# Rearranging the start and the tail of a fused attention and feed-forward block

## The chip, the cores and the metric

The kernel runs on one core of one Trainium2 chip. A core has five engines that run side by side: TensorE (PE in the profile; PEld is its weight load) multiplies matrices, VectorE (DVE) and ScalarE (ACT) do element work and can read the matmul results in PSUM, GpSimd (POOL) does element work in SBUF alone, and SyncE (SP) issues transfers. Each engine takes its instructions in the order in which the program lists them and waits at the first that isn't ready. The metric is the time of one execution on the device in microseconds (us).

## The reference, cut to what matters

The input x has 8 batches of 1024 rows and 256 columns. Everything is float32. From a small condition c come six rows per batch, used as shifts, scales and gates:

```python
mod = (silu(c) @ wmod).reshape(8, 6, 1, 256)
sa, ca, ga, sb, cb, gb = (mod[:, j] for j in range(6))
ga, gb = (sign(g) * maximum(abs(g), 0.25) for g in (ga, gb))   # sign of 0 is +1
h = layernorm(x) * (1 + ca) + sa
scores = einsum('nsd,ntd->nst', h * w_lhs, h * w_rhs)
x = x + ga * einsum('nst,ntd->nsd', softmax(scores, axis=2), h)
h = layernorm(x) * (1 + cb) + sb
x = x + gb * (relu(h @ W1 + b1) @ W2 + b2)                     # 256 -> 1024 -> 256
```

## The kernel before, in words

Rows are worked in tiles of 128, and tiles in halves of four: a batch b has eight tiles i and two halves g. One main loop runs over the batches and, within each, over the tiles. At step (b, i) it forms the scores of a tile two steps ahead and multiplies the finished weights of tile i with the values. From batch 1 on, each step also carries a share of the feed-forward of the half batch before. Batch 0 has no such work to mix in, and the last half batches are finished after the loop, in the tail.

**Statistics and normalised x.** `prepare_stats` takes mean and variance of a tile (two VectorE instructions), `prepare_rstd` the inverse deviation of a half (two on ScalarE), and `prepare_norm` writes the normalised tile into `xg`. In batch 0 it uses VectorE for half 0's first two tiles and GpSimd for all others; later batches use ScalarE.

**Turned operands.** The scores need rows as columns. `prepare_turn` makes the left operand `lT` on VectorE and the right one `rT` on ScalarE from the turned tile, for both 128-column parts k of the 256. In batch 0 the turning is done by TensorE into PSUM tiles `pth`; in batch 1 `prepare_blocks` does it by VectorE's block transposes and a round trip of transfers through DRAM (T_a to D_a to X_a or Y_early), so `prepare_turn` reads SBUF there.

**Scores and weights.** `direct` multiplies `lT` and `rT` into `psc`, and ScalarE copies it to `sc`. Both weights multiply element by element, so the scores are symmetric and only the upper triangle is computed; `mirror` fills the rest, in batch 0 (`mirror_first`) by TensorE transposes `ptm` and ScalarE copies. `row_max` finds a row's maximum, `max_turn` turns it (`pm`), `subtract` (VectorE) and `exponent` (ScalarE) give the weights `pT`; `product` multiplies them with `xg` into `po`, and `product_out` divides, adds to x and takes statistics.

**Modulation.** `mod_rows` multiplies the condition with `wmod`; `mod_columns` turns two of its rows into columns in a PSUM tile `pmc`. From these come `sides` (scales and shifts of the two operands) and `modT` (those of the second normalisation); `make_gcol` and `columns` do the like for the gate's and the bias's columns. Eight small VectorE operations make the gated rows `rows_sb`, which `first_rows` spreads over all partitions (`prow`) for batch 0. They are also stored to DRAM for the later batches.

**Feed-forward.** `pair_products`, `pair_sums` and `pair_last` compute the first layer for a pair of 128-unit chunks (c and c+4) with fewer products than the plain form; `kept` is a ScalarE copy of one product that the pair needs before its last matmul. `pair_relu` follows. In the tail, `second` multiplies the second layer plainly: for each of four row tiles, eight matmuls over the chunks in the order 0, 4, 1, 5, 2, 6, 3, 7. The first three row tiles are split: a first part, and later the rest.

**What sets the order.** The order on each engine is the order of the calls: `pin` fixes it. PSUM has eight banks, in pools of two (`ps_s`), two (`ps_t`) and four (`ps_a`); a new tile waits until the last user of the bank it is given is done.

Of the kernel before, what the change touches and what calls it, by code (L numbers as in the profile page):

```python
# [17 lines left out]
P = 128  # L18
# [6 lines left out]
def adaln_block_kernel(  # L25
# [161 lines left out]
    def mod_rows(part, parts):  # L187

        pm = ps_a.tile([P, HALF], F32, tag="a", name=f"pmr_{part}")
        w = parts * D  # L190
        for k in range(ND):
            nc.tensor.matmul(
                pm[:B, :w],
                lhsT=scT[:, k, :],
                rhs=wm[:, k, ds(part * D, w)],
                start=(k == 0),
                stop=(k == ND - 1),
            )
        nc.scalar.copy(
            mod[:, part : part + parts, :].rearrange("b s d -> b (s d)"), pm[:B, :w]  # L200
        )

    def mod_columns(part):

        pc = ps_t.tile([P, HALF], F32, tag="t", name=f"pmc_{part}")
        for j in range(2):
            for k in range(ND):
                nc.tensor.transpose(
                    pc[:, ts(j * ND + k, B)], mod[:, part + j, ts(k, P)], ident[:B, :B]
                )  # L210
        return pc[:, : 2 * ND * B].rearrange("p (j k b) -> p j k b", j=2, k=ND)
# [55 lines left out]
    def prepare_rstd(b, g):  # L267
        pre[b, g].append(rstd_of(pre[b, g][0], "ra", f"ra_{b}_{g}"))

    def prepare_norm(b, g):  # L270

        mv, r = pre.pop((b, g))
        if b > 0:
            shift = work.tile([P, TH], F32, tag="rs", name=f"rs_{b}_{g}")
            nc.vector.scalar_tensor_tensor(shift, mv[:, :, 0], -1.0, r, ALU.mult, ALU.mult)
        for j in range(TH):
            t = g * TH + j
            if b > 0:
                nc.scalar.activation(
                    xg_t[b][:, t, 0:D], x_tile(b, t), AF.Identity,  # L280
                    scale=r[:, j : j + 1], bias=shift[:, j : j + 1],
                )
                continue
            engine = nc.vector if t < TH // 2 else nc.gpsimd
            engine.tensor_scalar(  # L285
                xg_t[b][:, t, 0:D], x_tile(b, t), mv[:, j, 0:1], r[:, j : j + 1],
                ALU.subtract, ALU.mult,
            )
# [57 lines left out]
    def prepare_turn(b, g, vector=True):  # L346

        xg, pts = xg_t[b], []
        lT = lT_t[b, g] = two.tile([P, ND, HALF], F32, tag="lT", name=f"lT_{b}_{g}", bufs=2)
        rT = rT_t[b, g] = two.tile([P, ND, HALF], F32, tag="rT", name=f"rT_{b}_{g}", bufs=2)  # L350
        rows = lambda T, k: T[:, k, :].rearrange("p (t a v) -> p t a v", a=NV, v=V)
        for k in range(ND):
            if b > 0:
                pt = pre[b, g][:, k]
            else:
                pt = ps_t.tile([P, HALF], F32, tag="t", name=f"pth_{b}_{g}_{k}")
                for j in range(TH):
                    nc.tensor.transpose(pt[:, ts(j, P)], xg[:, g * TH + j, ts(k, P)], ident)
                pt = pt.rearrange("p (t a v) -> p t a v", a=NV, v=V)
            pts.append(pt)  # L360
            if vector:
                nc.vector.tensor_scalar(
                    rows(lT, k), pt, side_col(0, 0, k, b), side_col(0, 1, k, b),
                    ALU.mult, ALU.add,
                )
            nc.scalar.activation(
                rows(rT, k), pt, AF.Identity,
                scale=side_col(1, 0, k, b), bias=side_col(1, 1, k, b),
            )
        def left():  # L370
            for k in range(ND):
                nc.vector.tensor_scalar(
                    rows(lT, k), pts[k], side_col(0, 0, k, b), side_col(0, 1, k, b),
                    ALU.mult, ALU.add,
                )

        return left


# [62 lines left out]
    def mirror_first(i):  # L442
        sc = first_scores()
        j = i + 1
        while j < NT:
            n = min(TH, NT - j)
            pt = ps_t.tile([P, HALF], F32, tag="t", name=f"ptm_{i}_{j}")
            for q in range(n):
                nc.tensor.transpose(pt[:, ts(q, P)], sc[:, i, ts(j + q, P)], ident)
            nc.scalar.copy(  # L450
                sc[:, j : j + n, ts(i, P)],
                pt[:, : n * P].rearrange("p (q s) -> p q s", s=P),
            )
            j += n
# [3 lines left out]
    def row_max(b, i):  # L458
        m = work.tile([P, 1], F32, tag="m", name=f"m_{b}_{i}")
        nc.vector.tensor_reduce(m, score_row(b, i), AX.XY, ALU.max)  # L460
        max_t[b, i] = m
# [431 lines left out]
    out_t = {}  # L893
    order = [i for c in range(NH) for i in (c, c + NH)]

    def second(b, a, parts=(0, 1), cut=NI // 2):

        w2g, f = ffn["w2g"], ffn["f"]
        if 0 in parts:
            out_t[a] = ps_a.tile([P, HALF], F32, tag="a", name=f"py_{b}_{a}")  # L900
        py = out_t[a]
        for i in (order[:cut] if 0 in parts else []) + (order[cut:] if 1 in parts else []):
            nc.tensor.matmul(  # L903
                py[:, :D],
                lhsT=f[:, i, ts(a % TH, P)],
                rhs=w2g[:, i, :],
                start=(i == order[0]),
                stop=(i == order[-1]),
            )
# [29 lines left out]
    prepare_stats(0, 1, range(2, TH))  # L939
    make_sides()  # L940
    prepare_rstd(0, 1)
    prepare_norm(0, 1)
    prepare_turn(0, 0)
    mod_rows(2, 1)
    mod_rows(5, 1)
    direct(0, 0, range(1))
# [15 lines left out]
    nc.vector.tensor_tensor(rows_sb[:, 3, :], gate[:, 1, :], b2_row, ALU.mult)  # L962


    left()
    rows_tile(0)
    rows_d = dram.tile([B, 4, D], F32, name="rows_d")
    nc.sync.dma_start(out=rows_d, in_=rows_sb)
# [48 lines left out]
    def make_gcol():  # L1017
# [5 lines left out]
                )  # L1023
        nc.scalar.copy(gcol.rearrange("p j k b -> p (j k b)"), pg[:, : 2 * ND * B])

    pr = first_rows()
    direct(0, 0, range(1, 2))
    keep_rows(pr, 0)
    direct(0, 1, range(1, 2))
    xg_half = lambda g: nc.vector.tensor_tensor(  # L1030
# [2 lines left out]
        rows_t[0][:, 0:1, :].to_broadcast([P, TH, D]),  # L1033
        ALU.mult,
    )
    xg_half(0)
    row_max(0, 0)
    mirror(0, 0)
    xg_half(1)
    keep_rows(pr, 1)  # L1040
# [6 lines left out]
    mirror(0, 1)  # L1047
    exponent(0, 0)
    mod_rows(3, 2)
    make_gcol()  # L1050
    max_turn(0, 1)
    subtract(0, 1)
    while queue:
        spare()
    columns(b1_rows, 0)


    modT = const.tile([P, 2, ND, B], F32, name="modT")
    pmb = mod_columns(3)
    nc.vector.tensor_copy(modT[:, 0], pmb[:, 0])  # L1060
    nc.vector.tensor_scalar(modT[:, 1], pmb[:, 1], 1.0, None, ALU.add)

    def early(b, i):

        if b == 0:

            if i in (1, 2):
                prepare_rstd(1, i - 1)
            elif i == 5:
                ffn_rstd(0, 0)  # L1070
            if i in (2, 3):
                prepare_norm(1, i - 2)
                x_plus(1, i - 2)
            if i in (3, 4):
                xg_times(1, i - 3)
            elif i == 5:
                prepare_turn(1, 0)
                sum_w2()
            elif i == 6:
                load_x(2, 0)  # L1080
        else:
            if i == 2 and b + 1 < B:
                prepare_norm(b + 1, 0)
            elif i == 6 and b + 2 < B:
                load_x(b + 2, 0)
# [22 lines left out]
    def norms(b, i):  # L1108
        if b > 0 and i == 0:
            ffn_blocks(b - 1, 1)  # L1110
        if b == 0:
            if i == 0:
                prepare_start(1)
                prepare_stats(1, 0)
            elif i == 1:
                prepare_stats(1, 1)
                sum_w1()
        elif b + 1 < B:
            if i == 1:
                prepare_start(b + 1)  # L1120
                prepare_stats(b + 1, 0)
            elif i == 2:
                prepare_blocks(b + 1, 0)
                x_plus(b + 1, 0)
                xg_times(b + 1, 0)
        elif i == 4:

            ffn_blocks(b, 0)
        if b == B - 1:
            return  # L1130
        if i == 6:
            if b == 0:
                ffn_norm(b, 0)
            ffn_blocks(b, 0)
# [7 lines left out]
    for b in range(B):  # L1142
        for i in range(NT):
# [25 lines left out]
            if b == 0:  # L1169
# [18 lines left out]
                spare()  # L1188
                if ahead[0] == 0:
                    subtract(*ahead)  # L1190
                norms(b, i)
                spare()
                if i == NT - 1:
# [9 lines left out]
            if first:  # L1203
# [7 lines left out]
                    pair_relu(c - 1)  # L1211
                pair_sums(fb, fg, c)
                if (b, i) == (1, 0):
                    weights(*late)
                    late = None
                if ahead:
                    mirror(*ahead)
                pair_last(fb, fg, c)
# [7 lines left out]
                if i == 4 and b + 1 < B:  # L1226
                    prepare_blocks(b + 1, 1)
                    xg_times(b + 1, 1)
                if late:
                    subtract(*late)  # L1230
                pair_products(fb, fg, c + 1, (lambda: max_turn(*extra)) if extra else None)
                if (b, i) == (B - 1, TH):
                    ffn_rstd(b, 0)
                if i == 5:
# [114 lines left out]
    for g in range(NT // TH):  # L1349
# [24 lines left out]
        tiles = range(g * TH, (g + 1) * TH)  # L1374

        for a in tiles[:3]:
            second(b, a, (0,), NI - 2)
        for a in tiles:
            second(b, a, (0, 1) if a == tiles[3] else (1,), NI - 2)
            second_out(b, a)  # L1380
            spare()
            spare()
# [40 lines left out]
```

## Time and profile before

| | |
|---|---|
| time, median of 3 runs | 768.08 us (767.98 to 768.21) |
| time of the profiled execution | 768.33 us |
| its span in the profile | 766.5 us |
| TensorE busy | 756.5 us, 99% of the span |
| VectorE, GpSimd, ScalarE busy | 566.4, 539.3, 374.9 us |
| granted TensorE clock | 1.0 of full speed |

The span runs from the first to the last recorded instruction. A row of a timeline or a group gives start or total in us, the engine, the line of the kernel, the operation, and in square brackets how long the engine stood idle before it and which instruction ended that. The chain of waits follows the work that ended last backwards, from each instruction to what released it.

### The profile page before, as it was taken

How to read it: one execution, taken by the hardware profiler on the slowest of the kernel's cores; microseconds unless marked ns; L12 is line 12 of the kernel's file. 1: busy time of each engine (PE TensorE's matmuls, PEld its weight loads, DVE VectorE, ACT ScalarE, POOL GpSimd, SP SyncE). 2: the span in 40 equal slices, each digit the busy share in tenths (PEclk: the TensorE clock that was granted, in tenths of full speed). 3: DMA queues.
4: the chain of work that ended last, by engine and by line, in shares of the span. 5: the costliest groups of instructions: out<-in, count | busy, mean ns of one | idle time of the engine just before them, and what ended most of it. 6: DMA issues, size and time to landing. Idle time of an engine off the chain costs nothing.

```text
span 766.5 us, 11489 instructions
## 1 busy us (share of the span) xinstructions
PE 756.5 (99%) x3708; PEld 621.8 (81%) x3708; DVE 566.4 (74%) x1222; ACT 374.9 (49%) x681; POOL 539.3 (70%) x632
## 2 busy tenths in 40 slices
PE   8999999999999999999999999999999999999998
PEld 3577789888887888878888888988888788888886
DVE  6697779668796887858787787866879677594632
ACT  4464545635465355555536444563546535251511
POOL 4633975978859697687867788597884879469641
PEclk9999999999999999999999999999999999999999
DMA  5314434356343653535544544436535354152220
GB/s 194 124 39 142 122 104 121 107 186 172 93 130 107 186 148 112 148 103 160 145 123 117 151 151 131 111 116 187 171 91 131 104 160 129 42 143 72 82 83 27
DMA packets 106212, 95.18 MB, mean 124 GB/s; under 512 B 29701, under 2 KB 98849, under 8 KB 106153
## 3 DMA queue, kind: packets, MB, share of 16 engines
q1 hardware_dynamic: 98408, 85.81, 38.9%
q10 hardware_dynamic: 7744, 8.65, 3.8%
q8 instruction: 29, 0.48, 0.3%
q14 instruction: 31, 0.25, 0.1%
HBM read 50.62 MB, written 43.81 MB: 123 GB/s over the span
## 4 chain that ended last, share of the span: by engine, by line
PE 95%; DVE 2%; POOL 1%; DMA 1%; issue 1%; ACT 1%; SPq 0%; POOLq 0%; DVEq 0%
PE po L493 16%; PE psc L410 16%; PE pa L718 10%; PE pb L718 7%; PE pc L718 7%; PE yc L798 6%; PE ya L798 6%; PE yb L798 6%; PE pr L584 5%; PE pq L584 3%; PE pp L544 3%; PE py L903 3%; PE yd L798 3%; PE pm L465 1%; POOL xg L285 1%; DMA x<-in_L_attn_x_dram 1%
## 5 line engine op out<-in xcount | busy, mean ns | idle before, releaser
L772 POOL TENSOR_TENSOR f<-f,kept 128x512 f32<-128x512 f32 x64 | 81.5, 1275 | 101.9 <-DVE f L771 96.8
L410 PE MATMUL psc<-rT,lT 128*128 128x512 f32 (+3 forms) x384 | 134.8, 487 | 0.0
L493 PE MATMUL po<-xg,pT 128*128 128x257 f32 x576 | 131.6, 380 | 0.0
L493 PEld LDWEIGHTS po<-xg,pT 128*128 128x128 f32 x576 | 108.8, 190 | 16.0 <-issue 1.0
L410 PEld LDWEIGHTS psc<-rT,lT 128*128 128x128 f32 x384 | 67.5, 190 | 38.3 <-issue 25.3
L472 DVE TENSOR_TENSOR pT<-sc,pm 128x1024 f32<-128x1024 f32 x64 | 77.1, 1205 | 28.5 <-PE pm L465 22.0
L417 ACT COPY sc<-psc 128x512 f32<-128x512 f32 (+3 forms) x96 | 45.0, 476 | 103.5 <-PE psc L410 91.0
L481 ACT ACTIVATE pT<-pT 128x1024 f32<-128x1024 f32 x64 | 67.3, 1052 | 36.6 <-DVE pT L472 36.6
L460 DVE TENSOR_REDUCE m<-sc 128x1 f32<-128x1024 f32 x64 | 77.3, 1209 | 0.4 <-DMA sc<-D_m 0.4
L739 ACT COPY kept<-pa 128x512 f32<-128x512 f32 x64 | 37.4, 585 | 80.4 <-PE pa L718 80.4
L718 PE MATMUL pb<-hs,w1s 128*128 128x256 f32 x256 | 65.8, 379 | 0.0
L718 PE MATMUL pc<-hT,w 128*128 128x256 f32 x256 | 65.7, 379 | 0.0
L781 ACT ACTIVATE f<-f 128x512 f32<-128x512 f32 x64 | 40.1, 626 | 50.2 <-POOL f L772 50.1
L634 POOL TENSOR_TENSOR x<-x,rows 128x256 f32<-128x256 f32 x64 | 45.4, 743 | 22.3 <-DVE x L509 11.8
L718 PEld LDWEIGHTS pb<-hs,w1s 128*128 128x128 f32 x256 | 48.1, 190 | 7.5 <-DVE f L757 0.4
L718 PEld LDWEIGHTS pc<-hT,w 128*128 128x128 f32 x256 | 48.6, 190 | 6.6
L798 PE MATMUL yc<-f,w2s 128*128 128x256 f32 x224 | 52.1, 379 | 0.0
L798 PEld LDWEIGHTS yc<-f,w2s 128*128 128x128 f32 x224 | 41.5, 190 | 10.1 <-issue 2.9
L433 DVE STREAM_TRANSPOSE Tm<-sc 128x896 f32<-128x896 f32 (+6 forms) x49 | 34.7, 707 | 13.3 <-ACT sc L417 12.5
L791 POOL TENSOR_TENSOR ft<-f 128x256 f32<-128x256 f32 x56 | 41.0, 732 | 4.5 <-ACT f L782 4.4
L793 POOL TENSOR_TENSOR ft<-ft,f 128x256 f32<-128x256 f32 x56 | 40.9, 730 | 4.4
L792 POOL TENSOR_TENSOR ft<-ft,f 128x256 f32<-128x256 f32 x56 | 40.8, 729 | 4.4
(165 smaller groups left out, 1670.5 us busy)
## 6 DMA issues: line engine op xcount, KB each, us to landing
D_f<-T_f SPq DMA_DIRECT2D x60, 128.0 KB, 3.1
X_f<-D_f SPq DMA_DIRECT2D x15, 512.0 KB, 3.8
D_a<-T_a SPq DMA_DIRECT2D x56, 128.0 KB, 3.5
D_y<-T_y SPq DMA_DIRECT2D x56, 128.0 KB, 2.7
Y<-D_y SPq DMA_DIRECT2D x14, 512.0 KB, 4.0
out_dram<-x SPq DMA_DIRECT2D x14, 512.0 KB, 4.3
X_a<-D_a SPq DMA_DIRECT2D x13, 512.0 KB, 3.9
x<-in_L_attn_x_dram ACTq DMA_DIRECT2D x12, 512.0 KB, 4.2
```

What stands on the lines that cost most here:

```text
L410: nc.tensor.matmul(psc[:, : hi - lo], lhsT=lT_t[b, i // TH][:, k, ts(i % TH, P)], rhs=rT_t[b, n][:, k, lo - n * HALF : HALF], start=(k == ...
L417: nc.scalar.copy(score_row(b, i)[:, lo // V : hi // V, :], psc[:, : hi - lo].rearrange("p (n v) -> p n v", v=V),)
L460: nc.vector.tensor_reduce(m, score_row(b, i), AX.XY, ALU.max)
L472: nc.vector.tensor_tensor(pT.rearrange("p j (a v) -> p j a v", v=V), score_columns(b, i), pm[:, :P].rearrange("p (j a v) -> p j a v", j=1, ...
L481: nc.scalar.activation(pT_t[b, i], pT_t[b, i], AF.Exp)
L493: nc.tensor.matmul(po[:, : D + 1], lhsT=pT[:, t, :], rhs=xg_t[b][:, t, 0 : D + 1], start=(t == 0), stop=(t == NT - 1),)
L584: nc.tensor.matmul(out, lhsT=lhs[:, t, :], rhs=rhs[:, t, :], start=(t == 0), stop=(t == TH - 1),)
L634: queue.append(lambda: nc.gpsimd.tensor_tensor(out, in0, row, op))
L718: nc.tensor.matmul(out, lhsT=lhsT, rhs=rhs, start=True, stop=True)
L772: nc.gpsimd.tensor_tensor(f[:, c::NH, hi], f[:, c::NH, hi], kept[:, None, hi].to_broadcast([P, 2, H2]), ALU.add,)
L791: add(ft[:, 0, c], f[:, c + NH, hi], f[:, c, hi], ALU.subtract)
L798: nc.tensor.matmul(out, lhsT=lhs(c), rhs=rhs(c), start=(c == 0), stop=(c == NH - 1))
```

## The change

- `mod_columns` takes its PSUM tile from the pool of four instead of the pool of two, and so does the second of a row's two mirror transposes.
- In batch 0's second half, tiles 0 and 1 are normalised on VectorE instead of GpSimd, placed behind the turned operands of the first half.
- In `prepare_turn` with both operands, ScalarE takes the parts k in reversed order, so that it and VectorE read different banks. This call is used for batch 0's first half and for both halves of batch 1.
- The second score product of row 0 stands ahead of `prow`, and `row_max` of row 0 ahead of the first `xg_half`.
- The gate's columns, the bias's columns and `modT` are made inside the loop, behind the first attention product (step (0, 0)).
- Batch 1's second statistics are split over steps 1 and 2, and their `prepare_rstd` goes from step 2 to step 3.
- At step (1, 0), `exponent` goes behind the next pair's products.
- In the tail the first part of a row tile has four matmuls instead of six.

```diff
     def mod_columns(part):
-        pc = ps_t.tile([P, HALF], F32, tag="t", name=f"pmc_{part}")
+        pc = ps_a.tile([P, HALF], F32, tag="a", name=f"pmc_{part}")
...
-    def prepare_norm(b, g):
-        mv, r = pre.pop((b, g))
+    def prepare_norm(b, g, tiles=range(TH)):
+        mv, r = pre[b, g]
...
-        for j in range(TH):
+        for j in tiles:
...
-            engine = nc.vector if t < TH // 2 else nc.gpsimd
+            engine = nc.vector if j < TH // 2 else nc.gpsimd
...
             pts.append(pt)
+        def left(k):
+            nc.vector.tensor_scalar(
+                rows(lT, k), pts[k], side_col(0, 0, k, b), side_col(0, 1, k, b),
+                ALU.mult, ALU.add,
+            )
+        for k in range(ND):
             if vector:
-                nc.vector.tensor_scalar(
-                    rows(lT, k), pt, side_col(0, 0, k, b), side_col(0, 1, k, b),
-                    ALU.mult, ALU.add,
-                )
+                left(k)
+            q = ND - 1 - k if vector else k
             nc.scalar.activation(
-                rows(rT, k), pt, AF.Identity,
-                scale=side_col(1, 0, k, b), bias=side_col(1, 1, k, b),
+                rows(rT, q), pts[q], AF.Identity,
+                scale=side_col(1, 0, q, b), bias=side_col(1, 1, q, b),
             )
...
-            pt = ps_t.tile([P, HALF], F32, tag="t", name=f"ptm_{i}_{j}")
+            pool, tag = (ps_t, "t") if j == i + 1 else (ps_a, "a")
+            pt = pool.tile([P, HALF], F32, tag=tag, name=f"ptm_{i}_{j}")
...
-    def second(b, a, parts=(0, 1), cut=NI // 2):
+    def second(b, a, parts=(0, 1)):
...
+        cut = NI // 2
...
     prepare_rstd(0, 1)
-    prepare_norm(0, 1)
+    prepare_norm(0, 1, range(TH // 2, TH))
     prepare_turn(0, 0)
+    prepare_norm(0, 1, range(TH // 2))
...
+    direct(0, 0, range(1, 2))
     pr = first_rows()
-    direct(0, 0, range(1, 2))
...
+    row_max(0, 0)
     xg_half(0)
-    row_max(0, 0)
...
-    make_gcol()
     max_turn(0, 1)
     subtract(0, 1)
...
-    columns(b1_rows, 0)
     modT = const.tile([P, 2, ND, B], F32, name="modT")
-    pmb = mod_columns(3)
-    nc.vector.tensor_copy(modT[:, 0], pmb[:, 0])
-    nc.vector.tensor_scalar(modT[:, 1], pmb[:, 1], 1.0, None, ALU.add)
+    def make_columns():
+        make_gcol()
+        columns(b1_rows, 0)
+        pmb = mod_columns(3)
+        nc.vector.tensor_copy(modT[:, 0], pmb[:, 0])
+        nc.vector.tensor_scalar(modT[:, 1], pmb[:, 1], 1.0, None, ALU.add)
...
-            if i in (1, 2):
-                prepare_rstd(1, i - 1)
+            if i in (1, 3):
+                prepare_rstd(1, i // 2)
...
             elif i == 1:
-                prepare_stats(1, 1)
+                prepare_stats(1, 1, range(TH // 2))
                 sum_w1()
+            elif i == 2:
+                prepare_stats(1, 1, range(TH // 2, TH))
...
                 if ahead[0] == 0:
                     subtract(*ahead)
+                if i == 0:
+                    make_columns()
                 norms(b, i)
...
                 if (b, i) == (1, 0):
-                    weights(*late)
-                    late = None
+                    subtract(*late)
...
-                if late:
+                if late and (b, i) != (1, 0):
                     subtract(*late)
                 pair_products(fb, fg, c + 1, (lambda: max_turn(*extra)) if extra else None)
+                if (b, i) == (1, 0):
+                    exponent(*late)
+                    late = None
...
         for a in tiles[:3]:
-            second(b, a, (0,), NI - 2)
+            second(b, a, (0,))
         for a in tiles:
-            second(b, a, (0, 1) if a == tiles[3] else (1,), NI - 2)
+            second(b, a, (0, 1) if a == tiles[3] else (1,))
```

More of the change, by code (lines that the diff above doesn't have):

```diff
@@ L360, in prepare_turn @@
             pts.append(pt)
+        def left(k):
[4 more added lines that the diff above has]
+        for k in range(ND):
             if vector:
-                nc.vector.tensor_scalar(
-                    rows(lT, k), pt, side_col(0, 0, k, b), side_col(0, 1, k, b),
-                    ALU.mult, ALU.add,
-                )
+                left(k)
+            q = ND - 1 - k if vector else k
             nc.scalar.activation(
-                rows(rT, k), pt, AF.Identity,
-                scale=side_col(1, 0, k, b), bias=side_col(1, 1, k, b),
-            )
[L370 to L375, printed above, removed]
+                rows(rT, q), pts[q], AF.Identity,
+                scale=side_col(1, 0, q, b), bias=side_col(1, 1, q, b),
+            )
         return left
@@ L962, in adaln_block_kernel @@
     nc.vector.tensor_tensor(rows_sb[:, 3, :], gate[:, 1, :], b2_row, ALU.mult)
-    left()
+    for k in range(ND):
+        left(k)
     rows_tile(0)
```

## The prediction

> **What bounds the kernel now.** I read the page's engine table and the shares of the chain first, then the chain piece by piece, then the timelines of the first 70 us and the last 50. Page:
>
> ```profile
> span 766.5 us, 11489 instructions
> ...
> PE 756.5 (99%) x3708; PEld 621.8 (81%) x3708; DVE 566.4 (74%) x1222; ACT 374.9 (49%) x681; POOL 539.3 (70%) x632
> ...
> PE 95%; DVE 2%; POOL 1%; DMA 1%; issue 1%; ACT 1%; SPq 0%; POOLq 0%; DVEq 0%
> ```
>
> TensorE sets the time; only its few stalls can be won, since the change removes no matmul. The chain names the stalls in the prologue (start, duration, what), here up to the first attention product and where VectorE takes the chain over:
>
> ```profile
> 11.99 3.74 POOL xg L285 x3
> ...
> 26.09 0.55 ACT sc L450
> ...
> 28.98 0.57 ACT early_b L199
> ...
> 41.29 0.49 DVE x L509
> ...
> 45.70 1.10 DVE m L460
> ```
>
> The timeline shows who waits (start, duration, engine, line, operation, idle before it):
>
> ```profile
> 11.23 1.65 ACT L366 ACTIVATE rT<-pth,sides 128x512 f32<-128x512 f32 x2 [0.55 <-DVE lT L362]
> ...
> 15.77 0.76 PE L358 MATMUL pth<-ident,xg 128*128 128x128 f32 x5 [0.49 <-POOL xg L285]
> ...
> 46.95 0.29 PE L465 MATMUL pm<-ident,m 128*128 128x128 f32 x1 [0.36 <-DVE rl L507]
> ...
> 65.49 1.52 ACT L366 ACTIVATE rT<-X_a,sides 128x512 f32<-128x512 f32 x2 [2.97 <-DMA X_a<-D_a]
> ...
> 84.64 0.70 PE L718 MATMUL pa<-hT,w1s 128*128 128x256 f32 x2 [0.54 <-ACT kept L739]
> ```
>
> ScalarE's first turn starts the moment VectorE leaves the same bank (10.39+0.84=11.23). From 84.64 to the tail the chain is all TensorE but for a POOL stretch at 698.6 that the change leaves alone. The tail has two stalls:
>
> ```profile
> 723.97 12.50 PE L903 MATMUL py<-w2g,f 128*128 128x256 f32 x56 [0.69 <-ACT f L781]
> ...
> 750.73 12.44 PE L903 MATMUL py<-w2g,f 128*128 128x256 f32 x56 [0.44 <-ACT f L781]
> ```
>
> **What the skill says.** "PSUM — Partial Sum Buffer", PSUM bank collisions: accesses of two engines to one bank must be kept apart, read against read too. The 0.55 us wait agrees. "GPSIMD Engine Reference", Elementwise — side-by-side cycle accounting, has GpSimd about twice as slow as VectorE on a two-input add (4497 against 2293 ns); our one-tile normalisation shows the same ratio, 3.74/3=1.25 us on POOL against 1.17/2=0.58 on VectorE. "DMA: Bandwidth & Descriptors", Anatomy of one DMA, gives a fixed cost of some 2.0 us; here X_f lands 3.8 us after issue, so a late transposed block can't be caught up.
>
> **The change, part by part.** Issue paces from the trace: a 512-column matmul is two records of 0.43 us, a 256-column one two of 0.216, a 128-column transpose 0.108. All starts are TensorE's.
>
> (1) Banks apart, pmc in the other pool. Transposes of pth's second half no longer wait for sides (10.59); they follow the first at about 9.8. ScalarE ends ra at 10.69, turns k=1 to 11.53, then k=0 (VectorE leaves it at 11.23) to 12.36; VectorE does lT k=1 from 11.55 to 12.40. First score product 12.97 -> 12.42: **-0.55**.
>
> (2) Two tiles to VectorE. They run behind lT, 12.4 to 13.6; POOL's two end at 10.78+2x1.23=13.24; TensorE comes at 14.2 and doesn't wait. From 12.42 it has 1.72+0.86+1.30+1.72+0.86+1.72=8.18 us to the first mirror transposes: 20.66 (with 0.06 slip) against 21.95. **-0.74** more. The gate operations on VectorE start 0.15 later (13.62), so rows are ready at 17.04; prow now stands behind a score product, at 18.08, and is covered by 1.0. On SP the store of the rows waits for the same operations, and the reload of batch 1's rows and the loads of W1 and W2 stand behind it: all go 0.15 later. POOL first uses W1 behind its eight additions to x, which end near 29, some 9 us after W1's issue, so that is hidden; were it not, it would cost 0.15.
>
> (3) row_max ahead of xg_half, mirrors in both pools, mod's columns behind the product. Mirrors and scores take 0.77+2.58, so pm 0 goes at 24.01. Then 0.36 to VectorE, subtract 1.21, exponent 1.06, with 0.13 of hand-over: first product 26.77 against 30.50. VectorE's own queue (lT 17.5-19.0, row_max, two xg_half, row_max at a pace of 1.13) is free at 23.5; TensorE's (0.11+0.43+0.22+1.73+0.11) at 26.6; so both are hidden. **-2.44**.
>
> (4) The moved columns come after pm 2 (30.89): pt_g 0.45 with its latency, gcol copy 0.17 (behind the exponent, which ends at 31.15), pt_v 0.10, pmc 0.34, hand-overs 0.12: **+1.18** where before only pm stood. Behind pt_v's wait for the gcol copy stand pmc, the score products of row 3 and the second attention product; nothing else wants the bank. b1's columns come 1.8 us later than before, and their first reader on POOL is followed there by 12 us of idle. modT (0.16) on VectorE is hidden by its 1.4 us of idle before the next reciprocal.
>
> So pm 3 goes at 38.25 instead of 40.80.
>
> (5) Statistics split. pm 4 waited at 46.95 behind four statistics (4x0.53). With two, row_max ends at 43.2 and TensorE's 5.62 us (0.11+1.72+1.73+0.33+1.73) bring it to 43.87: **-0.53**. The other two stand in the next iteration, and what is late next is pm 7. From rl 2 (pm 4+0.20) VectorE had 46.79 to 60.72 with 0.41 idle; now it has 13.52+1.06=14.58 with none, and pm 7 follows by 0.13: pm 4+14.9, or 14.74 by pacing single rows. Before it was 13.92, of which TensorE needs 13.87. I take 14.74: pm 7 at 58.6, **+0.83**. The moved rstd (ScalarE 0.5) is ready 0.7 before VectorE asks. The normalised block it feeds is transposed at 53.6 instead of 55.86, and its DMAs on SP keep behind Y_early's read as before.
>
> (6) Reversed order of the turns, also in batch 1. There the sources lie in SBUF and nothing is gained; but rT's k=0, which the second score product reads first, now comes second. That product started at 66.36 on the first turn (65.49+0.8); now it needs both (65.49+1.52, read at 67.05). VectorE's and POOL's chains start from that product's copy, so all shift: **+0.69**. Bounds: 0 if the block lands 0.8 earlier relative to TensorE, 0.7 if not.
>
> (7) Exponent of (1,0) behind the next products. The kept copy then runs at 82.2 and the stall before 84.64 (about 0.7) goes. But the next kept copy (92.93-93.51) releases TensorE at 93.56, at the end of an unbroken ScalarE run since 87.30 that began with POOL's f (86.00), POOL being busy since hT. TensorE just comes there earlier and waits: **0**; bounds -0.6 to 0.
>
> (8) Tail in parts of four. Before, four matmuls (1.73) from 721.39 and 748.40 ended at 723.12 and 750.13, and TensorE stood until 723.97 and 750.73. Now 12 matmuls (5.19) stand ahead of chunk 2: 726.6 and 753.6 (on the old clock). The last ReLUs end at 726.40 and 753.16. **-0.85 -0.60**. The next half's pc would want POOL's hT at 736.94; it ends at 736.14, so the gain isn't lost there.
>
> Edits with no other user (popping pre, names) cost nothing. Sum: -0.55-0.74-2.44+1.18-0.53+0.83+0.69+0-1.45=-3.01. Span 763.5. The profiled execution took 768.33, 1.83 outside the span and 0.25 above the median 768.08: **765.1 us** on the median.
>
> **Rivals.** *All the lead arrives*: VectorE turns out not to bind up to pm 7 and the block lands early enough, so (5)+ and (6) cost nothing: 1.5 less, 763.6. For: VectorE had 0.41 idle there. Against: 24.09 busy of 26.10 us from 34.8 to 60.9.
> *Only the tail*: the early lead is eaten by VectorE (a late rl, pm 5 and pm 6 waiting too): 768.08-1.45=766.6. For: the chain runs on VectorE from 41 to 47 already. Against: it is fed by products that come earlier.
> *Only the prologue*: the tail meets another wait, such as a bank; 768.08-1.56=766.5. Against: the third tile's bank is freed at 723.5 and wanted at 724.85.
> *Slower*: the transposed block of batch 1. Its transposes come 4.9 us after those of the block before, instead of 5.34, so its writes overlap the other's read more. From the end of the transposes to landing took 65.49-57.15=8.34 us. Each us more delays psc at 66.36 and everything behind; at 3.0 more the gain is gone, at 3.5 more the time is 768.6. Against: SP issues in order, and the overlap grows by only 0.45.
>
> **How the numbers follow.** Forecast 0.65 (own range 764.3 to 766.0), all the lead 0.14, only the tail 0.12, only the prologue 0.06, slower 0.03. I call within 0.2% (1.54 us) what a measurement of this kernel can't tell from no change. Faster by more: 0.65+0.14 and a third of the prologue case, 0.81; within: 0.16; slower by over 0.2%: 0.03. The range runs from 763.5, so that it holds the full lead, to 766.4, short of the last three.
>
> **What would show it.** First score product near 12.4, first attention product near 26.8, pm 3 near 38.3 and pm 4 near 43.9 without a wait; pm 6 and pm 7 waiting for row_max, pm 7 near 58.6; psc waiting for the second rT turn; a TensorE wait on kept near 92; no ReLU wait in py. I'm wrong if pm 7 shows no wait (then faster), or if VectorE delays pm 5 by more than 0.3.

## The result, and the profile after

The changed kernel takes 765.59 us (median of 6 runs, 764.87 to 765.90) against 768.13 us for the kernel before, measured beside it (6 runs, 767.98 to 768.41). The ratio is 0.9965, 95% interval 0.9952 to 0.9978: 2.5 us less, more than the 0.2% (1.54 us) that the prediction takes for the least that can be told. The forecast was 765.1, range 763.5 to 766.4. The profiled execution took 765.59 us, 768.33 before.

The page of the kernel after, span, engines and shares of the chain:

```profile
span 763.7 us, 11487 instructions
...
PE 754.7 (99%) x3708; PEld 621.8 (81%) x3708; DVE 566.2 (74%) x1224; ACT 375.0 (49%) x681; POOL 535.2 (70%) x630
...
PE 88%; POOL 4%; DVE 3%; DMA 2%; issue 1%; ACT 1%; SPq 0%; DVEq 0%; POOLq 0%
```

TensorE still sets the time: it is busy for 99% of the span, with the same 3708 matmuls. VectorE has two operations more, GpSimd two fewer: the two normalised tiles. The timeline of the kernel after shows where TensorE stands now (start, duration, engine, line, operation; in brackets the idle before it and what ended it):

```profile
10.96 1.89 PE L192 MATMUL pmr<-wm,scT 128*8 128x256 f32 x8 [0.36 <-DMA wm<-in_L_wmod_dram]
24.51 0.82 PE L450 MATMUL ptm<-ident,sc 128*128 128x128 f32 x6
52.97 0.33 PE L450 MATMUL ptm<-ident,sc 128*128 128x128 f32 x1 [0.63 <-ACT sc L417]
64.00 1.52 ACT L373 ACTIVATE rT<-X_a,sides 128x512 f32<-128x512 f32 x2 [3.09 <-DMA X_a<-D_a]
65.57 4.99 PE L410 MATMUL psc<-rT,lT 128*128 128x512 f32 x12 [0.99 <-ACT rT L373]
92.77 0.70 PE L719 MATMUL pa<-hT,w1s 128*128 128x256 f32 x2 [0.69 <-ACT kept L740]
720.58 13.98 PE L905 MATMUL py<-w2g,f 128*128 128x256 f32 x64
746.48 13.98 PE L905 MATMUL py<-w2g,f 128*128 128x256 f32 x64
```

The output products of the tail (`py`) run without a wait; the stall near 84 us is gone and one of 0.69 stands at 92.77; the second score product of batch 1 starts at 65.57 behind both turns of `rT`. Below, "the block" is what these turns read: the second half of batch 1's normalised x, turned by VectorE and by the round trip through DRAM, which lands in X_a. The mirror transposes at 24.51 run on, where the kernel before waited for a copy:

```profile
26.69 0.44 PE L449 MATMUL ptm<-ident,sc 128*128 128x128 f32 x2 [0.68 <-ACT sc L450]
```

Three waits are new and were not foreseen: 0.41 for GpSimd's tile ahead of the transposes at 9.84, 0.36 for the second load of `wmod`, and 0.63 for the copy of score row 6.

Between marks that both traces have, each stretch from the mark of the row above (the last row apart), in us of TensorE's starts (pm i is the product that turns the maximum of score row i):

| stretch | before | after | difference | the prediction |
|---|---|---|---|---|
| to the first score product | 12.97 | 12.78 | -0.19 | -0.55 |
| to the first mirror transposes | 8.98 | 8.28 | -0.70 | -0.74 |
| to the first attention product | 8.55 | 6.18 | -2.37 | -2.44 |
| to pm 3 | 10.30 | 11.49 | +1.19 | +1.18 |
| to pm 4 | 6.15 | 5.63 | -0.52 | -0.53 |
| to pm 7 | 13.92 | 14.74 | +0.82 | +0.83 |
| to batch 1's second score product | 5.49 | 6.47 | +0.98 | +0.69 |
| to the first output product | 655.03 | 655.01 | -0.02 | 0 |
| the tail's two product stretches | 29.69 | 27.79 | -1.90 | -1.45 |

The sum is -2.71 against the forecast's -3.01. The first row counts from the span's start and holds chance too: `pmc`, which waits for the same ScalarE copy (of `cols`) in both kernels, started at 8.54 in this execution and at 8.96 in the one before. Two terms were too hopeful by 0.36 and 0.29, one too modest by 0.45.

### The profile page after: what moved, and what is told of

Same layout as the page of the kernel before. It is cut to its first block, busy times and chain, and to the rows that moved or that the text cites. A ratio compares the mean times of both kernels' runs of the same rounds, so it can differ in the third digit from the quotient of the medians.

```text
span 763.7 us, 11487 instructions
## 1 busy us (share of the span) xinstructions
PE 754.7 (99%) x3708; PEld 621.8 (81%) x3708; DVE 566.2 (74%) x1224; ACT 375.0 (49%) x681; POOL 535.2 (70%) x630
## 4 chain that ended last, share of the span: by engine, by line
PE 88%; POOL 4%; DVE 3%; DMA 2%; issue 1%; ACT 1%; SPq 0%; DVEq 0%; POOLq 0%
PE psc L410 15%; PE po L494 13%; PE pa L719 10%; PE pc L719 6%; PE pb L719 6%; PE yc L799 6%; PE ya L799 6%; PE yb L799 6%; PE pr L585 5%; PE py L905 4%; PE pq L585 3%; PE yd L799 3%; PE pp L545 3%; DMA wm<-in_L_wmod_dram 1%; PE pm L466 1%
## 5 line engine op out<-in xcount | busy, mean ns | idle before, releaser
L707 POOL TENSOR_TENSOR hs<-hT 128x256 f32<-128x256 f32 x16 | 11.6, 727 | 46.8 <-DVE hT L698 46.8
```

## The experiments

Every kernel was timed beside the kernel before, whose median stood between 767.75 and 768.14 us; so kernels are best compared by the ratio. Since runs of one kernel differ by 1 us and the intervals of most of these kernels overlap, the reading rests on the traces as well. **Span B** is the time from the first score product to the first output product: 708.42 in the kernel before, 707.80 after. It leaves out the loads at the start, and the tail. One trace of each kernel stands behind it, so small differences can be chance: tail_only has the same code as the kernel before in this whole stretch, and its span B is 0.30 shorter.

| kernel | first score product | span B | median us | ratio to before, 95% |
|---|---|---|---|---|
| tail_only | 12.75 | 708.12 | 766.05 | 0.9977 (0.9969-0.9986) |
| bank_shared | 12.93 | 707.99 | 765.85 | 0.9970 (0.9958-0.9982) |
| tiles_pool | 13.05 | 708.23 | 766.53 | 0.9984 (0.9978-0.9991) |
| wm_parts | 13.17 | 707.64 | 764.99 | 0.9961 (0.9949-0.9973) |
| cols_late | 13.26 | 706.68 | 764.60 | 0.9955 (0.9943-0.9967) |
| stats_whole | 13.15 | 706.66 | 764.68 | 0.9956 (0.9944-0.9969) |
| rs_pool | 12.12 | 707.86 | 765.06 | 0.9964 (0.9952-0.9976) |
| rt_plain | 13.06 | 707.33 | 764.73 | 0.9959 (0.9946-0.9973) |
| exp_ahead | 12.97 | 707.92 | 765.20 | 0.9968 (0.9956-0.9981) |
| combo1 | 12.74 | 706.20 | 764.02 | 0.9950 (0.9937-0.9962) |
| combo2 | 12.99 | 706.09 | 763.95 | 0.9947 (0.9935-0.9960) |
| combo3 | 12.33 | 706.07 | 763.56 | 0.9942 (0.9928-0.9955) |

**The tail alone (tail_only).** Kernel before, with

```diff
         for a in tiles[:3]:
-            second(b, a, (0,), NI - 2)
+            second(b, a, (0,))
         for a in tiles:
-            second(b, a, (0, 1) if a == tiles[3] else (1,), NI - 2)
+            second(b, a, (0, 1) if a == tiles[3] else (1,))
```

> The kernel before, with the tail alone changed: the output tiles' first parts take four chunks each instead of six. Theory (read from the trace of the changed kernel): the two stalls go and so do the small ReLU waits inside the old 14.92 us and 14.77 us stretches; each half takes about 13.9 us, together -1.9 us, so 766.2 us. The recorded step says -1.45, so 766.7. Rival: part of the tail's gain came only with the earlier start, or the next half meets another wait; then 767.2 or more. The prologue up to 66 us must stand as before.

Timeline of tail_only, the two output stretches:

```profile
720.87 13.98 PE L903 MATMUL py<-w2g,f 128*128 128x256 f32 x64
746.77 13.98 PE L903 MATMUL py<-w2g,f 128*128 128x256 f32 x64
```

The second follows the first by 25.90 us, as in the changed kernel (27.01 before): the tail's -1.90 owes nothing to the prologue. By the medians the edit alone wins 1.7 us, so it is some two thirds of the whole gain (0.67 by the medians, 0.70 by the traces).

**The statistics whole (stats_whole).** Changed kernel, with

```diff
-            if i in (1, 3):
-                prepare_rstd(1, i // 2)
+            if i in (1, 2):
+                prepare_rstd(1, i - 1)
...
-                prepare_stats(1, 1, range(TH // 2))
+                prepare_stats(1, 1)
                 sum_w1()
-            elif i == 2:
-                prepare_stats(1, 1, range(TH // 2, TH))
```

> The changed kernel, with the four statistics of batch 1's second half all in the second iteration, as before the change, and their rstd one iteration earlier. Theory (VectorE full from pm 4 to pm 7): pm 4 comes 0.5 later, near 44.9 us, with a wait for the row's maximum; pm 7 follows 13.9 behind instead of 14.74, near 58.8 us, so the split cost 0.3: 765.3. Rival: the split is a gain that arrives, since the transposed block decides at 65.57 and not pm 7; then 765.6 to 766.1.

Timeline of stats_whole (SPq is SP's queue of DMA issues):

```profile
45.27 0.29 PE L466 MATMUL pm<-ident,m 128*128 128x128 f32 x1 [0.37 <-DVE rl L508]
53.83 0.34 SPq L307 DMA_DIRECT2D Y_early<-D_a  x1
55.50 2.48 SPq L304 DMA_DIRECT2D D_a<-T_a  x4
63.23 1.52 ACT L373 ACTIVATE rT<-X_a,sides 128x512 f32<-128x512 f32 x2 [2.38 <-DMA X_a<-D_a]
```

and of the kernel after:

```profile
54.20 0.34 SPq L307 DMA_DIRECT2D Y_early<-D_a  x1
55.41 3.07 SPq L304 DMA_DIRECT2D D_a<-T_a  x4
```

pm 4 waits again and comes 6.16 behind pm 3; pm 7 follows 13.92 behind pm 4. From the first score product to pm 7 that is 46.04 against 46.32: the -0.3 that was expected. But span B fell by 1.14. The rest, 0.86, lies in the transposed block: it landed 4.04 after pm 7 instead of 4.90.

The second block's four writes are issued 1.67 us behind the first block's read, where the kernel after leaves 1.21, and they are issued in 2.48 us instead of 3.07. Thirteen of the fourteen traces fall in two groups, whose times overlap a little. With whole statistics the two block transposes on VectorE begin 5.34 us apart, and from the issue of the second's writes to its landing it takes 7.73 to 8.31 us (six kernels, mean 8.02, the kernel before at 8.31); split, they begin 4.87 apart and it takes 8.25 to 8.83 (seven, mean 8.59). The fourteenth, rs_pool, has them 4.78 apart and 8.78. So the split costs 0.3 on VectorE and a further 0.57 in the DMAs, on the mean; in this trace, with the shortest trip of all (7.73), it is 0.86. The medians can't tell these sizes apart: the gain over the kernel before is 3.07 us here and 2.54 in the changed kernel.

**The shift on GpSimd (rs_pool).**

```diff
-            nc.vector.scalar_tensor_tensor(shift, mv[:, :, 0], -1.0, r, ALU.mult, ALU.mult)
+            if (b, g) == (1, 1):
+                nc.gpsimd.tensor_tensor(shift, mv[:, :, 0], r, ALU.mult)
+                nc.gpsimd.tensor_scalar(shift, shift, -1.0, None, ALU.mult)
+            else:
+                nc.vector.scalar_tensor_tensor(
+                    shift, mv[:, :, 0], -1.0, r, ALU.mult, ALU.mult
+                )
```

> The changed kernel, with the shift of batch 1's second half computed on GpSimd (two small operations) instead of behind the block transposes on VectorE, so that ScalarE's four normalisations start about 0.8 earlier and the copy of score row 6 is not behind them. Theory: the mirror transpose at 52.97 loses its 0.63 wait, but VectorE is full from pm 4 to pm 7, so pm 7 waits for the row's maximum by as much instead: 765.5. Rival: that 0.63 wait was the cause of the late pm 7, then 765.0.

Timeline of rs_pool:

```profile
52.04 0.33 PE L456 MATMUL ptm<-ident,sc 128*128 128x128 f32 x1 [0.35 <-ACT sc L423]
...
58.35 0.29 PE L472 MATMUL pm<-ident,m 128*128 128x128 f32 x1 [0.22 <-DVE m L467]
```

The wait at the mirror shrinks from 0.63 to 0.35 and one of 0.22 appears at pm 7 for the row's maximum. From pm 4 to pm 7 it takes 14.65 instead of 14.74: VectorE, not ScalarE's copy, sets this stretch. Span B did not fall.

**The right side in its old order (rt_plain).**

```diff
-            q = ND - 1 - k if vector else k
+            q = ND - 1 - k if vector and b == 0 else k
```

> The changed kernel, with the right side's turns of batch 1 in their old order (chunk 0 first). Theory: the second score product of batch 1 starts on the first turn, near 64.8 us instead of 65.57, still waiting about 0.4 for the block's landing at 64.0; everything behind moves, so -0.75 us: 764.8. Rival: the lead is lost again behind it (at the copy of kept near 92 us, or VectorE), then 765.6.

Timeline of rt_plain:

```profile
64.50 1.52 ACT L373 ACTIVATE rT<-X_a,sides 128x512 f32<-128x512 f32 x2 [3.10 <-DMA X_a<-D_a]
...
65.37 4.99 PE L410 MATMUL psc<-rT,lT 128*128 128x512 f32 x12 [0.50 <-ACT rT L373]
```

The product starts 0.87 behind the landing instead of 1.57: 0.70 won, and all of it stays: from there to the first output product it takes 655.02 us, 655.01 in the changed kernel. Span B fell by 0.47 only, since the block took 8.81 in this execution (8.59 after).

**The columns later (cols_late).** Only b1's columns stay at step 0; gate's and mod's go to the end of step 5, behind pm 7; some 5 us later TensorE meets the wait for the block.

```diff
-        pg = ps_t.tile([P, HALF], F32, tag="t", name="pt_g")
+        pg = ps_a.tile([P, HALF], F32, tag="a", name="pt_g")
...
     def make_columns():
-        make_gcol()
-        columns(b1_rows, 0)
         pmb = mod_columns(3)
+        make_gcol()
...
                 if i == 0:
+                    columns(b1_rows, 0)
+                elif i == 5:
                     make_columns()
```

> The changed kernel, with the columns of gate and of mod moved from the end of the first iteration to that of the sixth, both in banks of the accumulators' pool, where TensorE waits 0.99 us for the transposed block anyway; only b1's columns stay. Theory: behind pm 2 TensorE loses about 0.15 instead of 1.18, pm 3 comes near 37.7 instead of 38.73, VectorE has the room to follow (it idles 1.49 us there), and the block of batch 1 comes a full 1.0 earlier; the moved transposes cost about 0.7 inside a wait: 764.6. Rival: the block's round trip or VectorE takes the gain up, 765.6; or the moved columns delay the batch's first product by more than the wait hides, 765.9.

From pm 2 to pm 3 it takes 6.53 instead of 7.46; the moved work makes pm 7 to the next score product 4.38 instead of 3.60, inside the wait. Span B fell by 1.12: the 0.93, and some 0.15 because the block took 8.44 in this execution (8.59 after). So the prologue was one chain from pm 2 to the landing.

**The two tiles back on GpSimd (tiles_pool).**

```diff
-            engine = nc.vector if j < TH // 2 else nc.gpsimd
+            engine = nc.vector if t < TH // 2 else nc.gpsimd
```

> The changed kernel, with the two tiles that went to VectorE back on GpSimd. Theory: GpSimd ends its four tiles at about 15.3 us, the second block's transposes wait for it, and the first mirror transposes go at about 21.8 instead of 21.06: +0.7 there. If the prologue to 65.57 us is one chain, all of it arrives: 766.3. Rival: slack before the transposed block takes it up, 765.6.

Timeline of tiles_pool:

```profile
15.72 0.98 PE L358 MATMUL pth<-ident,xg 128*128 128x128 f32 x7 [0.57 <-POOL xg L285]
```

The wait for GpSimd is back and the mirror transposes come 9.07 behind the first score product instead of 8.28: +0.79. Of this, 0.43 is left in span B; the block landed 0.34 sooner after its writes in this execution (8.25). By span B this lies between the theory (+0.7) and its rival (0); the median, 766.53, is on the theory's side (766.3) and past it. Two of its 22 executions took 769.4 and 769.9 us, which stays unexplained.

**The exponent in its old place (exp_ahead).**

```diff
                 if (b, i) == (1, 0):
-                    subtract(*late)
+                    weights(*late)
+                    late = None
...
-                if late and (b, i) != (1, 0):
+                if late:
                     subtract(*late)
...
-                if (b, i) == (1, 0):
-                    exponent(*late)
-                    late = None
```

> The changed kernel, with the exponent of batch 1's second row back ahead of the next pair's products. Theory (the recorded step): the stall near 84 us is back, about 0.7, and the wait for the copy of kept near 92.8 us is gone: 765.6, no difference. Rival: the edit was worth its stall, 766.3.

Timeline of exp_ahead:

```profile
84.17 0.70 PE L719 MATMUL pa<-hT,w1s 128*128 128x256 f32 x2 [0.54 <-ACT kept L740]
```

That stall is back and the later one is gone. From batch 1's second score product to the first output product it takes 655.00 us, 655.01 in the changed kernel: nothing.

**The first score product (bank_shared, wm_parts).** `bank_shared` puts pmc back in the transposes' pool:

```diff
-        pc = ps_a.tile([P, HALF], F32, tag="a", name=f"pmc_{part}")
+        pool, tag = (ps_t, "t") if part == 0 else (ps_a, "a")
+        pc = pool.tile([P, HALF], F32, tag=tag, name=f"pmc_{part}")
```

> The changed kernel, with the first columns of mod (pmc) back in the pool of the transposes, so that the second half of the first block's transposes waits for VectorE's reads of that bank. Recorded step: the first score product comes 0.55 later. Theory now: what stands in front of that product is TensorE's own row (the transposes, then 1.82 us of the small products) and wmod's second load; from pmc to the first score product it took 3.19 us where the load was in time and up to 4.24 where it was not, so the shared bank costs 0.35 in the first case (3.54) and nothing in the second. Everything from the first score product to the end stands as in the changed kernel: 765.6 to 766.0.

`wm_parts` cuts wmod's load:

```diff
-    nc.sync.dma_start(out=wm[:, :, 2 * D : 6 * D], in_=wmod_v[:, :, 2 * D : 6 * D])
+    for lo_, hi_ in ((2, 3), (5, 6), (3, 5)):
+        nc.sync.dma_start(
+            out=wm[:, :, lo_ * D : hi_ * D], in_=wmod_v[:, :, lo_ * D : hi_ * D]
+        )
```

> The changed kernel, with the second load of wmod cut in three: the two column blocks that the first products read go first, the two that are read at 25 us last; the same bytes, two more transfers on SP. Theory: the product pmr no longer waits for that load (0.36 us at 10.96), the first score product starts at about 12.4 instead of 12.78, and what is won there arrives at the end: 765.2. Rival 1: the smaller loads land no earlier, 765.6. Rival 2: the first score product moves but the rows' operations or the transposed block hold the later stretch, 765.6.

With the shared bank the first score product came 3.48 behind pmc. With banks apart and no wait for the load it was 3.18 to 3.21 (five traces): by this one trace the shared bank costs 0.3. In the product's start it isn't seen: 12.75 to 12.97 in the three traces with the bank shared, 12.12 to 13.26 in the eleven with banks apart. Nor is the wait of the kernel before a fixed price. tail_only has the same prologue, but `sides` was done 0.94 behind pmc's start there and not 1.48, and its timeline shows no wait of the transposes:

```profile
9.55 1.37 PE L358 MATMUL pth<-ident,xg 128*128 128x128 f32 x8
10.92 1.89 PE L192 MATMUL pmr<-wm,scT 128*8 128x256 f32 x8
12.75 1.98 PE L410 MATMUL psc<-rT,lT 128*128 128x512 f32 x4
```

`wm_parts` settled nothing: no wait for the load in its trace, but none either in exp_ahead, stats_whole, tiles_pool and rs_pool, which have the one load. In most of these pmc itself was late (9.78 to 9.98, 8.91 in rs_pool), for another reason. Timeline of the kernel after, and then of exp_ahead:

```profile
5.99 1.88 PE L192 MATMUL pmr<-wm,scT 128*8 128x512 f32 x4
```

```profile
6.63 2.49 PE L192 MATMUL pmr<-wm,scT 128*8 128x512 f32 x4
```

The same four products take 1.88 us or up to 2.69.

**Together (combo1, combo2, combo3).** `combo1` is stats_whole and rt_plain, `combo2` adds cols_late, `combo3` adds wm_parts.

> The changed kernel with the statistics whole again and batch 1's right side turned in its old order. Theory: the block transposes stand 5.34 us apart again, so the second block lands about 8.0 after its transposes instead of 8.6, and the second score product starts on the first turn; TensorE is then hardly idle there. From the first score product to the first output product 706.4 us, against 707.8 in the changed kernel and 706.7 with the statistics alone: 764.2. Rival: the two do not add, since TensorE itself decides once the block is in time; then as the statistics alone, 764.7.

> As the run before, and the columns of gate and mod moved to the sixth iteration as well. Theory: pm 3 and all behind it come 0.93 earlier, but the moved transposes stand for 0.75 in a stretch in which TensorE no longer waits, so 0.2 is won: 706.2 us from the first score product to the first output product, 764.0. Rival: the wait that hid them comes back, since the block is late again, and all of the 0.93 is won: 763.3.

> As the run before (statistics whole, right side's turns in the old order, columns moved), and wmod's second load in three parts with the two that are read first ahead. In the two runs before, TensorE waited 0.22 and 0.64 us for that load in front of pmr, and the first score product came 3.84 and 4.46 us after pmc. Theory: the parts land in time, no wait for wm is left, the first score product comes 3.2 us after pmc, and the rest of the kernel stands: 706.1 us from there to the first output product; 763.6. Rival: pmc itself comes later in this execution, as it did in five of the earlier ones, and the time stays at 764.0.

Timeline of combo1:

```profile
62.37 6.60 PE L410 MATMUL psc<-rT,lT 128*128 128x512 f32 x16
```

Timeline of combo2:

```profile
58.31 0.41 PE L208 MATMUL pmc<-ident,early_b 8*128 8x8 f32 x4
58.58 0.39 PE L1025 MATMUL pt_g<-ident,early_c 8*128 8x8 f32 x4
```

In combo1 batch 1's score products run on without the wait, so the columns moved there in combo2 are no longer hidden: 0.93 less from pm 2 to pm 3, 0.79 more from pm 7 to the next score product. Span B fell by 0.11 only. Timeline of combo3:

```profile
9.82 0.77 PE L361 MATMUL pth<-ident,xg 128*128 128x128 f32 x5 [0.30 <-POOL xg L288]
10.51 1.89 PE L195 MATMUL pmr<-wm,scT 128*8 128x256 f32 x8
12.33 1.55 PE L413 MATMUL psc<-rT,lT 128*128 128x512 f32 x3
```

Here pmc came early (8.63) and the load was in time: the first score product comes 3.70 behind pmc (3.84 and 4.46 in combo1 and combo2, with waits of 0.22 and 0.64 for the load). The expected 3.2 was missed, since GpSimd's second tile now holds the transposes by 0.30. That the parts made the load timely isn't shown: rs_pool, with the one load, had it at 9.76 and its first score product at 12.12. At 763.56 us it beats both kernels: 4.6 us below the kernel before, 2.0 below the changed one (the kernel before stood at 768.14 and 768.13 beside the two).

## Why the prediction was right, and where not

**Step (1), banks apart: mis-sized.** "First score product 12.97 -> 12.42" took the turned operands as what comes last (12.36 and 12.40). The term that failed is TensorE's own queue, which the step put at nothing: the products pmr stand ahead of the score product, and in all fourteen traces it starts 1.82 us behind their start, to 0.01. In the kernel before they came behind the transposes' wait for `sides`:

```profile
10.59 0.63 PE L358 MATMUL pth<-ident,xg 128*128 128x128 f32 x4 [0.63 <-DVE sides L223]
11.15 1.89 PE L192 MATMUL pmr<-wm,scT 128*8 128x256 f32 x8
```

With that wait gone they met wmod's second load, which landed at 10.91; so the product starts at 12.78, though the operands were ready at 12.26. The -0.19 isn't the price of the edit either: from pmc the product came 4.24 us later, 4.01 before. For the bank itself bank_shared shows 0.3, no trace 0.55.

**Steps (2) to (4): right.** -0.70, -2.37 and +1.19 against -0.74, -2.44 and +1.18. tiles_pool and cols_late move these stretches by +0.79 and -0.93. Step (3), the largest, has no run of its own; its parts are read from the two traces. Of the 2.37, 1.47 lies between pmr and the first attention product, where the columns stood, and 1.19 of it comes back at pm 3, as step (4) said. The other 0.90 lies between pm 0 and pmr, where the mirror's wait of 0.68 was. What `row_max` ahead of `xg_half` gave alone wasn't measured. One price of step (2) was a slow one: two tiles took VectorE 1.17 us in the kernel before and 0.70 to 0.87 in the other traces, so that it is some three times as fast as GpSimd (1.22 us a tile) there, not twice.

**Step (5): right in size, wrong in place.** -0.52 and +0.82 (-0.53 and +0.83). "pm 6 and pm 7 waiting for row_max" was to show it, and "if pm 7 shows no wait" stands among the signs of being wrong. Pm 7 shows none, and the time went where it was forecast all the same: the row-6 mirror waited 0.63 for a copy that stands on ScalarE behind four normalisations, which wait for `rs` behind VectorE's block transposes. rs_pool shows the prediction's cause to hold: with that wait cut, pm 7 waits.

**Step (6): mechanism right, one term left out.** The order cost 0.70 (0.69 predicted; rt_plain). The other 0.28 is the round trip, which took 8.59 us where the kernel before had 8.31:

```profile
57.18 2.00 SPq L304 DMA_DIRECT2D D_a<-T_a  x4
```

The step gave 0.7 as its upper bound and left the trip out; the rival "slower" named the rest, said that "the overlap grows by only 0.45", and the forecast gave that no price. The growth is right (4.87 apart instead of 5.34), and 0.57 more of trip goes with it on the mean of thirteen traces, 0.28 between these two. A single pair says little: tail_only, the same code up to there as the kernel before, had 7.96. So the split of the statistics, +0.30 by the sum of step (5), costs nearly 0.9 on the mean. That overlapping transfers are the reason is argued from order and times; the transfers themselves were not pulled apart by any other edit.

**Step (7): right.** exp_ahead shows it, 0.01 us.

**Step (8): mis-sized.** "-0.85 -0.60" counted the stall ahead of each long record. The records themselves held more: 723.97 to the next product at 736.31 is 12.34 us for 56 matmuls of 0.216, 12.10. So 0.24 were waits too short to be shown alone, and in the other half, where 0.79 went (14.77 less 13.98), 0.19 were outside the counted stall. What such a stretch can give is its length less its work: 1.10 (14.92 less 13.82) and 0.79.

**The rivals.** "All the lead" fell: it was lost at pm 3 to pm 7 and at the block, as worked out. "Only the tail" fell at the first attention product. "Only the prologue" fell with tail_only.

**What set off what.** The prologue gave 0.81 where 1.56 was predicted, the tail 1.90 where it was 1.45. The medians agree: 2.54 us for the whole change less 1.70 for the tail alone leaves 0.84. That the time came out within 0.5 us of the forecast is luck in part, because these errors have opposite signs.

## What to carry to other kernels

Where an engine is full over several steps, moving its work from one of them to the next won nothing here, and it shifted the transfers that hang on that engine: ask how far apart two transfers start, before and after. Ask also what stands ahead of a product on its own engine: an operand that is ready earlier helps only when that is done. Size a stall by a stretch's length less its work, not by the waits that the profile prints. Small work goes best where the bound engine waits anyway, but that place is gone once the wait is mended: the two gains don't add.

## What was not expected of the hardware

The first score product's start differs by about 1 us between traces: 12.12 to 13.26 in the eleven of kernels with banks apart, which are nearly alike up to there. The loads are one part: wmod's second load, where it is one, landed between 9.76 and 11.40. TensorE's pace at the start is another. pmr's first four products start 0.43 us apart in the kernel after, but 0.82, 0.85 and then 0.43 in wm_parts, where the pace changes at 8.3 us. They took 1.87 to 1.92 us in nine traces and 2.17 to 2.69 in five, while the granted clock reads 1.00 in both. The Trainium skill has this in "TensorE: Matmul & The Clock Gate", Part 1: The HAM clock gate: the array starts at half its clock, until a window of about 3.4 us that runs free of the kernel's start has been busy. The traces agree in the factor of two and in that the time of the change varies. No run here was made to change it.
